# A graph network of three layers: twenty placed ranges per chunk instead of 22, and a second gather of 128 rows per four chunks

## The chip, the cores and the metric

The kernel runs on one core of one Trainium2 chip. The metric is the device time of one execution in microseconds; a smaller one is better. The engines are named as in the profile: PE (TensorE, matmuls, with PEld for its weight loads), DVE (VectorE), ACT (ScalarE), POOL (GpSimd, which issues the gathers here) and SP (SyncE, which issues the plain DMAs).

## The reference

6250 nodes with 64 features, 206250 edges sorted by their target node. Three layers of attention over the edges, a residual, and a final normalization:

```
for i in range(3):
    q, k, v = x @ Wq + bq, x @ Wk + bk, x @ Wv + bv
    e = edge_attr @ We
    alpha = sum(q[dst] * (k[src] + e)) / sqrt(64)
    p = exp(alpha - segment_max(alpha, dst)[dst])
    w = p / segment_sum(p, dst)[dst]
    x = relu(segment_sum((v[src] + e) * w, dst) + x @ Ws + bs)
    if i < 2: x = layer_norm(x)
out = layernorm(x_in + log_softmax(x))
```

The part that matters here is `x[src]`: for each edge, the row of 64 numbers of its source node.

## The kernel before

The edges are cut into 403 chunks of 512, a chunk into four tiles of 128 edges (`T = 4`), and four chunks make a batch (`LB = 4`), which is also the unit of work: 100 full batches and a rest. For each unit the program computes scores (`scores`, line 1641), exponentials (`exps`, ACT), transposes of the probabilities (`weights`, PE, then a copy to `probT`), and weighted sums (`sums`, line 1679).

The source rows of a chunk come in two ways. **By gather:** an indirect DMA on POOL fetches 128 rows of 64 numbers (`take`, line 592). **By matmul:** while the first layer runs, a sorter (`sorter`, `Move`) puts the edges of each chunk into a new order. The nodes are 49 blocks of 128. A chunk has a number of *ranges* (`WINDOWS`) of sixteen *places* (`SL`) each; range h holds only edges whose source lies in blocks 2h to 2h+3 (`BW = 4`). Edges that find no place in a range stand behind, in the order they had. With 22 ranges 352 places are filled so: tiles 0 and 1 wholly, and 96 rows (`PART`) of tile 2. In layers two and three the rows of placed edges are then selected by matmuls and not gathered:

- `Picker.aim` (line 1301): VectorE makes four one-hot tables `hot` from a key table (line 1313), for a pair of ranges and sixteen chunks (four batches, `TURN`).
- `Picker.bank` (line 1336): PE multiplies the node blocks `halves` with them, eight matmuls of 256 columns (line 1352); ACT casts the result into `kept` (line 1360). This is one *job*. `PAIRS` says how many pairs a layer has: 6 in the first layer, 11 in the others. Pair q is due with the batch k for which q % 4 == k % 4, so a batch has two or three jobs.
- `Picker.naturals` (line 1366): PE brings the selected rows into edge order, a matmul per tile and chunk with `kept` as weights (line 1387); DVE copies them to the batch's tile `feat`.

What is not placed is gathered (`rows_wanted`, line 575): per batch in layers two and three four gathers of tile 3, one per chunk, and one gather of 128 rows into `few` that serves the last 32 rows of tile 2 of all four chunks. `settle` (line 607) copies `few` into place on ACT, 32 rows per chunk. A gather's index is first copied to a small tile `gate` by ACT (`release`, line 631), which paces the gathers: those of batch u+2 are released at points inside unit u.

The order in each engine's queue is written by hand. A unit of layers two and three runs `scores` of the unit before, `naturals` of the next unit, one job, transposes of the rows (`turn`), the transposes of the probabilities, the remaining jobs, the sums, the settling copies.

The places come from `ranking` (line 892), four times, each for up to 112 chunks at once: one step per kind of source range, with four matmuls (line 927), an ACT copy with bias (931) and DVE operations. The first ranking must end before any chunk can be sorted. `REACH` bounds, per tile, the places that edges of this tile may take; the sorter's matmuls (lines 1063 and 1077) have this many columns. `Move.index` (line 1108) writes the node numbers of the edges to be gathered into `src_b`. A general computation (`general_path`) follows only if some chunk's edges don't fit the ranges or reaches.

Of the kernel before, what the change touches and what calls it, by code (L numbers as in the profile page):

```python
# [19 lines left out]
P = 128  # L20
# [16 lines left out]
WINDOWS = 22  # L37
# [14 lines left out]
REACH = (392, 416, 456, CH)  # L52
# [383 lines left out]
def main_path(  # L436
# [96 lines left out]
    assert 2 * (WINDOWS - 1) + BW < NB <= 2 * BINS and NT % TURN == 0 and U0 % TURN == 0 and REST * LB == P  # L533
# [22 lines left out]
    def fetch(layer, k):  # L556

        c0, m = batches[k]
        feat = feats.tile([P, LB * T * 2 * D], F32, name="feat")
        if placed(layer, k):  # L560
            nc.sync.dma_start(feat[:, LB * T * D :], eaP[k])
        if layer or placed(layer, k):
            feat = feat.rearrange("p (h c t d) -> p c t h d", h=2, c=LB, d=D)
        else:
            feat = feat.rearrange("p (c t h d) -> p c t h d", h=2, c=LB, d=D)
        if not placed(layer, k):
            nc.sync.dma_start(
                feat[:, :m, :, 1].rearrange("p c t d -> p (c t) d"),
                ea[c0 : c0 + m].rearrange("c (t p) d -> p (c t) d", p=P),
            )  # L570
        loaded[layer, k] = feat
        if layer and placed(layer, k):
            spares[layer, k] = later.tile([P, D], F32, name="few", bufs=FB + 1)

    def rows_wanted(layer, k):
# [6 lines left out]
        return [(None, 0)] + [(c, T - 1) for c in range(m)]  # L582

    def indices(layer, k, c, t):
# [3 lines left out]
        if c is None:  # L588
            return src_b, k * LB * T + (2 * LB - 1 if layer else LB + 1 + t // 2)
        return src_b, k * LB * T + t * LB + c  # L590

    def take(layer, k, c, t, index):

        nc.gpsimd.indirect_dma_start(  # L594
            out=loaded[layer, k][:, c, t, 0] if c is not None else spares[layer, k] if layer else loaded[0, k][:, t, 1, 0],
# [11 lines left out]
    def settle(layer, k):  # L607

        if layer and placed(layer, k):
            for c in range(LB):  # L610
                nc.scalar.copy(
                    loaded[layer, k][PART:, c, 2, 0], spares[layer, k][c * REST : (c + 1) * REST, :]
                )
# [396 lines left out]
    class Move:  # L1010
# [97 lines left out]
        def index(self):  # L1108
# [929 lines left out]
```

## Time and profile before

| what | us |
|---|---|
| median of 3 runs (4546.31 to 4551.62) | 4548.02 |
| the profiled execution, time | 4547.86 |
| the profiled execution, span from first to last instruction | 4546.1 |
| PE busy in the span (82%) | 3750.4 |
| DVE busy (68%) | 3110.5 |
| POOL busy (56%) | 2547.7 |
| ACT busy (54%) | 2434.5 |

The mean granted clock of TensorE is 0.895. A row of the groups view reads: source line, engine, operation, output<-inputs, shapes, count, then busy us and mean ns of one, then the idle time of the engine just before such instructions and what ended it. Matmuls overlap, so the busy time of a group divided by its count is less than the mean length of one. A row of the windows view gives, for one stretch, its length, the busy us of the five engine columns with the number of instructions, the granted clock, the share of the DMA engines' time and GB/s. In the timeline each row is a start, a duration, an engine and an operation.

### The profile page before, as it was taken

How to read it: one execution, taken by the hardware profiler on the slowest of the kernel's cores; microseconds unless marked ns; L12 is line 12 of the kernel's file. 1: busy time of each engine (PE TensorE's matmuls, PEld its weight loads, DVE VectorE, ACT ScalarE, POOL GpSimd, SP SyncE). 2: the span in 40 equal slices, each digit the busy share in tenths (PEclk: the TensorE clock that was granted, in tenths of full speed). 3: DMA queues.
4: the chain of work that ended last, by engine and by line, in shares of the span. 5: the costliest groups of instructions: out<-in, count | busy, mean ns of one | idle time of the engine just before them, and what ended most of it. 6: DMA issues, size and time to landing. Idle time of an engine off the chain costs nothing.

```text
span 4546.1 us, 106920 instructions
## 1 busy us (share of the span) xinstructions
PE 3750.4 (82%) x35698; PEld 2635.5 (58%) x35698; DVE 3110.5 (68%) x8905; ACT 2434.5 (54%) x6979; POOL 2547.7 (56%) x2094
## 2 busy tenths in 40 slices
PE   5778888888888888888789888888878888888885
PEld 2445555555555555555477666666747666666664
DVE  5566676776766766666477777777746777777784
ACT  2334544544545444544456666666645666666674
POOL 5545566666665665655265655565526655565653
PEclk9788998988989899998789999999878988899997
DMA  5446666667666677776467767777646776777774
GB/s 114 113 125 174 172 177 182 169 177 184 173 172 184 166 188 192 189 185 178 136 154 183 191 168 191 187 178 183 172 112 142 182 175 170 181 182 184 176 186 97
DMA packets 827547, 766.85 MB, mean 169 GB/s; under 512 B 395281, under 2 KB 624935, under 8 KB 826990
## 3 DMA queue, kind: packets, MB, share of 16 engines
q1 hardware_dynamic: 666370, 565.02, 49.8%
q0 software_dynamic: 66688, 68.42, 8.2%
q10 hardware_dynamic: 93932, 126.48, 7.9%
q8 instruction: 288, 4.72, 0.4%
q14 instruction: 269, 2.20, 0.2%
HBM read 599.30 MB, written 160.27 MB: 167 GB/s over the span
## 4 chain that ended last, share of the span: by engine, by line


## 5 line engine op out<-in xcount | busy, mean ns | idle before, releaser
L594 POOL DMA_INDIRECT feat<-in_x,gate x1044 | 1278.7, 1225 | 896.3 <-ACT gate L631 622.0
L1313 DVE TENSOR_SCALAR hot<-key,rank 128x512 fp32r<-128x512 f16 (+2 forms) x2832 | 1165.5, 474 | 144.4 <-DMA key<-keyS 34.6
L594 POOL DMA_INDIRECT feat<-x,gate x816 | 946.3, 1160 | 533.7 <-ACT gate L631 225.3
L1638 ACT COPY featT<-ps_a 64x512 f32<-64x512 f32 x1176 | 682.8, 581 | 86.3 <-remote 21.8
L1352 PE MATMUL ps_x<-hot,halves 128*128 128x256 f32 (+2 forms) x4368 | 684.1, 306 | 19.9 <-ACT kept L1360 9.0
L1352 PEld LDWEIGHTS ps_x<-hot,halves 128*128 128x128 f32 x4368 | 598.0, 202 | 31.8 <-ACT kept L1360 19.1
L1063 PE MATMUL ps_x<-hit,rest 128*64 128x512 bf16 (+3 forms) x3200 | 501.1, 391 | 11.0 <-issue 10.7
L1687 PE MATMUL ps_g<-feat,probT 128*32 128x128 f32 x9672 | 403.2, 295 | 117.7 <-issue 53.0
L594 POOL DMA_INDIRECT few<-x,gate x198 | 283.8, 1433 | 366.1 <-ACT gate L631 138.5
L1655 DVE TENSOR_REDUCE most<-ps_s 128x1 f32<-128x512 f32 x297 | 204.1, 687 | 391.3 <-PE ps_s L1648 156.6
L1052 DVE TENSOR_SCALAR hit<-ruler,pos 128x512 bf16<-128x512 f16 (+3 forms) x1600 | 421.6, 334 | 13.3 <-PE ps_m L1077 12.4
L1360 ACT CAST kept<-ps_x 128x512 fp32r<-128x512 f32 (+2 forms) x546 | 307.3, 582 | 218.1 <-PE ps_x L1352 137.0
L1648 PE MATMUL ps_s<-featT,q 128*32 128x512 f32 x2376 | 405.6, 640 | 11.2 <-issue 7.2
L1687 PEld LDWEIGHTS ps_g<-feat,probT 128*32 128x32 f32 x9672 | 287.1, 117 | 197.4 <-issue 104.5
L1635 PE MATMUL ps_a<-ident,feat 128*128 128x128 f32 x2348 | 353.1, 288 | 41.8 <-ACT gate L631 11.1
L1063 PE MATMUL ps_x<-hit,raw 128*64 128x512 bf16 (+3 forms) x1600 | 332.9, 404 | 8.0 <-issue 7.8
L631 ACT COPY gate<-src_b 128x1 int32<-128x1 int32 x1946 | 325.8, 191 | 20.7 <-ACT eN L1103 15.6
L1635 PEld LDWEIGHTS ps_a<-ident,feat 128*128 128x128 f32 x2348 | 288.6, 149 | 63.8 <-issue 23.2
L1387 PEld LDWEIGHTS ps_m<-twice,kept 128*128 128x128 f32 x1600 | 213.2, 206 | 186.9 <-issue 186.6
L1662 ACT ACTIVATE prob<-ps_s,part 128x512 f32<-128x512 f32 x297 | 204.3, 688 | 185.2 <-issue 33.2
L1063 PEld LDWEIGHTS <-rest 128*64 128x64 bf16 x3200 | 206.5, 123 | 162.3 <-issue 80.1
L1695 ACT COPY part<-ps_g 128x128 f32<-128x128 f32 (+1 forms) x309 | 82.6, 267 | 394.1 <-remote 124.9
(253 smaller groups left out, 5587.3 us busy)
## 6 DMA issues: line engine op xcount, KB each, us to landing
feat<-eaP SPq DMA_DIRECT2D x292, 512.0 KB
featT<-eaS SPq DMA_DIRECT2D x292, 512.0 KB
key<-keyS SPq DMA_DIRECT2D x668, 128.0 KB
raw<-in_ea SPq DMA_DIRECT2D x200, 256.0 KB
eaS<-eT ACTq DMA_DIRECT2D x200, 256.0 KB
eaP<-eN ACTq DMA_DIRECT2D x200, 256.0 KB
to<-toS SPq DMA_DIRECT2D x292, 128.0 KB
part<-part SPq DMA_DIRECT2D x600, 32.5 KB
```

The costliest lines, as they stand in the source:

```text
L594: nc.gpsimd.indirect_dma_start(out=loaded[layer, k][:, c, t, 0] if c is not None else spares[layer, k] if layer else loaded[0, k][:, t, 1, 0],
L631: copy(gate, index[:, i : i + 1])
L1052: nc.vector.tensor_scalar(hit, ruler[:, : REACH[t]], self.pos[:, at : at + 1], None, ALU.is_equal)
L1063: nc.tensor.matmul(self.px[i][j * D : (j + 1) * D, : REACH[t]], self.part(i, part)[:, (j * T + t) * D : (j * T + t + 1) * D], self.hits[t, ...
L1313: nc.vector.tensor_scalar(hot[:, a:b].rearrange("p k w e -> p (k w e)"), self.keys[job][:, a * 2 * SL : b * 2 * SL], rank[:, h : h + 1], None,
L1352: nc.tensor.matmul(px[:, w, a:b], halves[block >= EARLY][:, block - EARLY * (block >= EARLY)].rearrange("p h d -> p (h d)"), made[h][:, a: ...
L1360: nc.scalar.copy(kept[t][:, a:b, at : at + 2 * SL].rearrange("p k (w e) -> p w k e", w=2), px[:, :, a:b])
L1387: nc.tensor.matmul(pn[:, t - ts[0], c], kept[t][:, k % TURN * LB + c], twice, start=True, stop=True)
L1635: nc.tensor.transpose(pt[:, j - js[0], t // 2], rows[:, t * D : (t + 2) * D], ident)
L1638: nc.scalar.copy(featT[:, :, :, h, :], pt[h * D : (h + 1) * D])
L1648: nc.tensor.matmul(self.p_s[rows], self.q[:, j * STRIDE : j * STRIDE + W], self.featT[:, j, :], start=False, stop=True)
L1687: nc.tensor.matmul(p_g[rows, :].rearrange("n (h d) -> n h d", h=2), self.probT[:, t, rows], batch[:, c + j, t], start=(t == 0), stop=(t == ...
```

## The change

`WINDOWS` goes from 22 to 20, and what follows from it: 320 placed edges per chunk, 64 placed rows in tile 2 (`PART`), 64 rows to be gathered there (`REST`), ten pairs in layers two and three (`PAIRS`). `few` becomes two gathers' worth of rows, one gather of 128 rows for two chunks; the settling copies become two, each for two chunks; `index` writes one more column of node numbers per batch. The reaches are set anew.

```diff
-WINDOWS = 22
+WINDOWS = 20
...
-REACH = (392, 416, 456, CH)
+REACH = (376, 408, 464, CH)
...
-            spares[layer, k] = later.tile([P, D], F32, name="few", bufs=FB + 1)
+            spares[layer, k] = later.tile([P, LB // 2, D], F32, name="few", bufs=FB + 1)
...
-        return [(None, 0)] + [(c, T - 1) for c in range(m)]
+        return [(None, c) for c in range(0, m, 2)] + [(c, T - 1) for c in range(m)]
...
-            return src_b, k * LB * T + (2 * LB - 1 if layer else LB + 1 + t // 2)
+            return src_b, k * LB * T + LB + t // 2 + (LB // 2 if layer else 0)
...
-            out=loaded[layer, k][:, c, t, 0] if c is not None else spares[layer, k] if layer else loaded[0, k][:, t, 1, 0],
+            out=loaded[layer, k][:, c, t, 0] if c is not None else spares[layer, k][:, t // 2] if layer else loaded[0, k][:, t, 1, 0],
...
-            for c in range(LB):
-                nc.scalar.copy(
-                    loaded[layer, k][PART:, c, 2, 0], spares[layer, k][c * REST : (c + 1) * REST, :]
-                )
+            for i in range(2):
+                nc.scalar.copy(loaded[layer, k][PART:, i::2, 2, 0], spares[layer, k][i * REST : (i + 1) * REST])
...
-            pi = pa[:, : 3 + 2 * LB]
+            pi = pa[:, : 3 * LB]
...
-                at = 3 + (t - 2) * LB
+                at = (t - 1) * LB
...
+                rows = slice(c % 2 * REST, (c % 2 + 1) * REST)
+                at = (LB + c) // 2
                 nc.tensor.matmul(
-                    pi[c * REST : (c + 1) * REST, 2:3], self.to[:, SLOTS : 3 * P], pickc[:, c : c + 1], start=True, stop=True
+                    pi[rows, at : at + 1], self.to[:, SLOTS : 3 * P], pickc[:, c : c + 1], start=True, stop=True
                 )
             nc.vector.tensor_scalar(
-                src_b[:, k * LB * T + LB + 1 : (k + 1) * LB * T], pi, float(N - 1), None, ALU.min
+                src_b[:, k * LB * T + LB : (k + 1) * LB * T], pi, float(N - 1), None, ALU.min
             )
```

The rows below are the engines' programs in order, each with its line, operation, output<-inputs and output shape, repeated rows counted as x8. First PE in layer two, the last rows of a unit that prepares a batch with k % 4 == 2, before: two jobs (8 matmuls each, here over two halves of the node blocks) stand between the transposes of the probabilities (L1674) and the sums (L1687).

```order
L1648 MATMUL ps_s<-featT,q 32x512 x4
L1387 MATMUL ps_m<-twice,kept_254 128x64 x4
L1387 MATMUL ps_m<-twice,kept_32446 128x64 x4
L1387 MATMUL ps_g<-twice,kept_32447 96x64 x4
L1352 MATMUL ps_x<-hot,halves 128x256 x8
L1635 MATMUL ps_a<-ident,feat 128x128 x8
L1674 MATMUL ps_p<-ident,prob 128x128 x4
L1352 MATMUL ps_x<-hot,halves 128x256 x6
L1352 MATMUL ps_x<-hot,halves_32445 128x256 x10
L1687 MATMUL ps_g<-feat,probT 32x128 x16
```

The same place now:

```order
L1648 MATMUL ps_s<-featT,q 32x512 x4
L1387 MATMUL ps_m<-twice,kept_254 128x64 x4
L1387 MATMUL ps_m<-twice,kept_32350 128x64 x4
L1387 MATMUL ps_g<-twice,kept_32351 64x64 x4
L1352 MATMUL ps_x<-hot,halves 128x256 x8
L1635 MATMUL ps_a<-ident,feat 128x128 x8
L1674 MATMUL ps_p<-ident,prob 128x128 x4
L1352 MATMUL ps_x<-hot,halves 128x256 x6
L1352 MATMUL ps_x<-hot,halves_32349 128x256 x2
L1687 MATMUL ps_g<-feat,probT 32x128 x16
```

One job is left there, and the matmuls for tile 2 write 64 rows, not 96. In the other three of four units only the latter differs.

ACT in layer two, from the settling copies of one unit to those of the next, before (`gate` copies release gathers, `featT` are the copies behind `turn`):

```order
L611 COPY feat<-few 32x64 x4
L1662 ACTIVATE prob,part<-ps_s,part 128x512
L631 COPY gate<-src_b 128x1
L1360 CAST kept_254<-ps_x 128x2x16x16
L1638 COPY featT<-ps_a 64x4x128
L631 COPY gate<-src_b 128x1
L1638 COPY featT<-ps_a 64x4x128 x2
L631 COPY gate<-src_b 128x1
L1638 COPY featT<-ps_a 64x4x128
L1360 CAST kept_32446<-ps_x 128x2x16x16
```

The same stretch now:

```order
L611 COPY feat<-few 64x2x64 x2
L1662 ACTIVATE prob,part<-ps_s,part 128x512
L629 COPY gate<-src_b 128x1 x2
L1360 CAST kept_254<-ps_x 128x2x16x16
L1638 COPY featT<-ps_a 64x4x128 x2
L629 COPY gate<-src_b 128x1
L1638 COPY featT<-ps_a 64x4x128 x2
L629 COPY gate<-src_b 128x1
L1360 CAST kept_32350<-ps_x 128x2x16x16
```

Both gathers into `few` are now released at the unit's first point, and a gate copy more stands in the queue; POOL issues two gathers into `few` and four into `feat` per batch, where it issued one and four. The gathers of a layer's first batch have no gate and go one after the other: five before, six now.

More of the change, by code (lines that the diff above doesn't have):

```diff
@@ L532, in main_path @@
     U0 = LEAD
-    assert 2 * (WINDOWS - 1) + BW < NB <= 2 * BINS and NT % TURN == 0 and U0 % TURN == 0 and REST * LB == P
+    assert 2 * (WINDOWS - 1) + BW < NB <= 2 * BINS and NT % TURN == 0 and U0 % TURN == 0 and 2 * REST == P
     EARLY = -(-(2 * (2 * PAIRS[0] - 1) + BW) // GS) * GS
```

## The prediction

> **What bounds the kernel now.** I read the page's first part, then the busy times by stage, then the groups of TensorE, then single units of work.
>
> ```profile
> span 4546.1 us, 106920 instructions
> PE 3750.4 (82%) x35698; PEld 2635.5 (58%) x35698; DVE 3110.5 (68%) x8905; ACT 2434.5 (54%) x6979; POOL 2547.7 (56%) x2094
> ```
>
> The profiled execution took 4547.86 us, 1.8 us more than its span, and stands 0.16 us under the median of the runs shown; the sum below is made against 4547.9. PE leads with 82%, but the share is a mean over stages. The next view cuts the span at the layer boundaries; its columns are the stretch, its length, busy us of PE, PE's weight loads, DVE, ACT and POOL (instructions in brackets), granted clock, DMA share, GB/s.
>
> ```profile
> 300.00:2200.00 1900.00, 1583.07 (x15411) 976.14 (x15409) 1275.37 (x4052) 926.57 (x2662) 1142.03 (x922) 0.90 0.67 178
> 2200.00:2300.00 100.00, 77.56 (x534) 57.63 (x530) 51.86 (x172) 39.93 (x94) 15.50 (x9) 0.68 0.38 103
> 2300.00:3330.00 1030.00, 906.16 (x8937) 706.89 (x8937) 767.07 (x1914) 642.74 (x1877) 598.62 (x488) 0.93 0.73 180
> 3330.00:3440.00 110.00, 77.85 (x495) 59.68 (x493) 53.86 (x165) 40.34 (x113) 30.71 (x25) 0.64 0.39 95
> 3440.00:4440.00 1000.00, 851.97 (x8535) 677.35 (x8532) 743.40 (x1882) 647.03 (x1854) 576.21 (x473) 0.93 0.74 179
> ```
>
> In the first layer PE is busy 83% at clock 0.90. In the second and third (rows three and five, the stretches I call steady) it is busy 88% and 85% at 0.93, with DVE at 74%, ACT at 63%, POOL at 58%. The two changes of layer (rows two and four) run at 0.68 and 0.64: short, and chained. So PE is nearest to the end nearly everywhere, and an edit is worth mostly the PE work it removes, less what PE then waits longer. What PE does and waits for in the steady stretches:
>
> ```profile
> L1352 PE MATMUL ps_x<-hot,halves 128*128 128x256 f32 x4183 | 654.5, 305 | 19.9 <-ACT kept L1360 9.0 <-DVE hot L1313 7.3 <-issue 3.3
> L1687 PE MATMUL ps_g<-feat,probT 128*32 128x128 f32 x6200 | 248.2, 287 | 82.4 <-DVE probT L1677 47.3 <-issue 33.2 <-DVE hot L1313 0.8
> L1674 PE MATMUL ps_p<-ident,prob 128*128 128x128 f32 x780 | 128.3, 290 | 69.5 <-ACT prob L1662 64.4 <-issue 5.0
> ```
>
> The first row is the selection matmuls: 4183 took 654.5 us, so a job of eight takes 1.25 us, with hardly any waiting (19.9 us). The other two show where PE does wait: the transposes of the probabilities for ScalarE's exponentials (64.4 us), the sums for VectorE's copy of the transposed probabilities (47.3). A job stands just ahead of each; it is also cover for those waits, and that is what keeps its removal from paying in full.
>
> **Part 1: a selection job less per four batches.** Pairs of ranges per batch group fall from 11 to 10 in layers two and three. The pair removed belongs to every fourth group start, 26 times in a layer, 52 in all. Each takes with it eight matmuls (1.25 us of PE), four one-hot comparisons, a cast of the result and a key load. The kernel already holds the experiment: of four successive units three have three jobs and one has two, and afterwards it is two and two. I cut the steady stretches into units, at the first matmul of each unit's scores, and summed those with no node-finishing matmuls in them, the 30 two-job units first, the 85 three-job units second (first row, last row, sum):
>
> ```profile
> 2341.65:2349.69 8.04, 7.72 (x93) 5.93 (x85) 7.09 (x18) 6.11 (x20) 4.79 (x6) 1.00 0.89 226
> ...
> 4423.87:4432.47 8.60, 6.99 (x87) 5.92 (x89) 6.21 (x15) 5.76 (x19) 4.21 (x5) 1.00 0.71 181
> sum 287.45, PE 240.88 PEld 190.93 DVE 212.54 ACT 185.51 POOL 155.77; mean PE 8.03 PEld 6.36 DVE 7.08 ACT 6.18 POOL 5.19
> ```
>
> ```profile
> 2308.72:2320.28 11.56, 10.73 (x101) 8.65 (x92) 6.69 (x17) 6.49 (x20) 7.08 (x8) 0.85 0.63 154
> ...
> 4413.70:4423.87 10.17, 9.80 (x99) 6.94 (x91) 8.81 (x23) 6.54 (x21) 6.16 (x6) 1.00 0.74 173
> sum 894.08, PE 788.39 PEld 632.71 DVE 637.85 ACT 568.45 POOL 490.04; mean PE 9.28 PEld 7.44 DVE 7.50 ACT 6.69 POOL 5.77
> ```
>
> A unit takes 287.45/30 = 9.58 us with two jobs and 894.08/85 = 10.52 with three: 0.94 us for a job, of which PE's busy time (8.03 against 9.28) explains 1.25, so three quarters of the PE time removed comes back as time. With all 46 and 141 whole units, node-finishing ones too, the sums are:
>
> ```profile
> sum 446.32, PE 376.07 PEld 290.82 DVE 347.19 ACT 287.92 POOL 265.35; mean PE 8.18 PEld 6.32 DVE 7.55 ACT 6.26 POOL 5.77
> ```
>
> ```profile
> sum 1548.00, PE 1354.08 PEld 1071.78 DVE 1139.19 ACT 981.28 POOL 893.75; mean PE 9.60 PEld 7.60 DVE 8.08 ACT 6.96 POOL 6.34
> ```
>
> That is 9.70 and 10.98: 1.28 us a job. The three-job units hold more finishing steps (56 of 141 against 16 of 46), so I stay near the first: 1.0 us, **52 us** for 52 jobs, with ends 49 and 67. DVE's four comparisons, ACT's cast and the key load ran beside PE and are worth nothing more; they are inside the measured difference.
>
> **Part 2: narrower natural-order matmuls.** The third tile's placed part shrinks from 96 to 64 columns of weights, for 800 matmuls in layers two and three. The first layer does the same operation with 64 already:
>
> ```profile
> L1387 PE MATMUL ps_g<-twice,kept 128*96 128x64 f32 x800 | 108.8, 262 | 13.1 <-ACT part L1695 8.4 <-issue 4.4 <-DVE sk L1432 0.2
> L1376 PE MATMUL ps_p<-twice,kept 128*64 128x64 f32 x368 | 36.9, 223 | 1.6 <-issue 1.6
> ```
>
> 108.8/800 = 0.136 us against 36.9/368 = 0.100: 0.036 x 800 = 29 us of PE. At three quarters, as in part 1, **22 us** (ends 0, if all of it turns into waiting for the exponentials behind it, and 29). The copy to SBUF that follows keeps its length per partition, so it costs the same.
>
> **Part 3: fewer ranking steps.** Each of four rankings counts 21 kinds, not 23. The first ranking stands ahead of all sorting; five steps of it in this stretch (PE of that line alone):
>
> ```profile
> 86.60:97.20 10.60, 6.51 (x20) 3.20 (x20) 1.00 0.31 70
> ```
>
> 20 matmuls in 10.60 us: a step takes 2.1 us there and 1.30 us of PE. In the first ranking the steps form a chain over PE, ACT and DVE, so two fewer give 4.2 us whole. The six others lie beside other work: 6 x 1.30 x 0.75 = 6. Together **10 us** (4 to 12).
>
> **Part 4: the reaches of the products.** The widths per tile go from 392, 416, 456, 512 to 376, 408, 464, 512: 16 columns fewer in 1776.
>
> ```profile
> L1063 PE MATMUL ps_x<-hit,rest 128*64 128x392 bf16 x800 | 105.3, 339 | 1.5 <-issue 1.3
> L1063 PE MATMUL ps_x<-hit,rest 128*64 128x456 bf16 x800 | 121.1, 375 | 5.6 <-issue 5.4
> ```
>
> 15.8 us for 64 columns over 800 matmuls; the undivided words add half as many matmuls. 15.8 x 1.5 x 16/64 = 6 us of PE, at three quarters **4 us** (0, and 10 if time is proportional to the width).
>
> **Part 5: the sorter a move earlier.** With four fewer steps in the first ranking, moves begin earlier: in the program order two moves are left after the first layer's loop, not three counted from its last unit's scores. The tail runs with idle PE:
>
> ```profile
> 2190.00:2220.00 30.00, 21.32 (x199) 11.06 (x198) 9.75 (x37) 9.54 (x20) 5.29 (x5) 0.75 0.33 109
> 2260.00:2290.00 30.00, 24.89 (x101) 21.73 (x102) 21.01 (x67) 8.57 (x19) 7.25 (x5) 0.50 0.34 83
> ```
>
> In the first row PE idles 8.7 us of 30. I take **3 us** (0 to 8.7).
>
> **Part 6: a sixth gather per batch, and its gate and settling copies.** 200 more gathers of 128 rows on POOL.
>
> ```profile
> L594 POOL DMA_INDIRECT feat<-x,gate x816 | 946.3, 1160 | 533.7 <-ACT gate L631 225.3 <-issue 149.3 <-ACT feat L611 134.9
> L594 POOL DMA_INDIRECT few<-x,gate x198 | 283.8, 1433 | 366.1 <-ACT gate L631 138.5 <-DVE feat L1394 72.3 <-PE ps_x L1352 44.3
> ```
>
> A unit's POOL time goes from 4 x 1.16 + 1.43 = 6.1 us to 7.5, in units of 9.6 to 11. The gathers released in a unit feed the unit after the next, so 1.4 us later is hidden by a whole unit; I cost them at nothing there. If that cover were gone, PE would wait for rows. At the two changes of layer there is no such lead: the six gathers of the first batch go one after the other, and the last ones end PE's wait:
>
> ```profile
> 2287.08 6.41 DVE L1313 TENSOR_SCALAR hot<-key,rank 128x512 fp32r<-128x512 f16 x16
> 2286.80 6.82 POOL L594 DMA_INDIRECT feat<-x,src_b  x1 [0.30 <-issue]
> 2295.96 0.33 PE L1635 MATMUL ps_a<-ident,feat 128*128 128x128 f32 x1 [1.55 <-DMA feat<-x,src_b]
> ```
>
> The fifth gather here took 6.82 us, beside sixteen one-hot comparisons that VectorE ran without a break from 2287.08 for 6.41 us; TensorE then waited 1.55 us for its rows. A sixth adds one gather length, 1.16 to 1.43 us, at each change of layer: **-2.5 us** (0, since the last job before it is gone as well, to -8 if two are caught by the comparisons). The Trainium skill's "SBUF — State Buffer", section "Who interferes with whom", says that a VectorE operation in a two-port mode locks GpSimd out of a shared port for its whole length, and that software descriptors wait for it; the row of 6.82 us agrees. Nothing of the sum hangs on it.
>
> ScalarE: four settling copies become two of twice the length.
>
> ```profile
> L611 ACT COPY feat<-few 32x64 f32<-32x64 f32 x800 | 193.2, 241 | 18.9
> L631 ACT COPY gate<-src_b 128x1 int32<-128x1 int32 x1946 | 325.8, 191 | 20.7 <-ACT eN L1103 15.6 <-issue 4.1 <-ACT eT L1091 0.9
> L1695 ACT COPY part<-ps_g 128x128 f32<-128x128 f32 x300 | 80.4, 268 | 384.3 <-remote 124.9 <-PE ps_s L1648 66.2 <-PE ps_g L1687 54.2
> ```
>
> Two copies of 128 elements at about 0.268 (the nearest row of that length) replace four of 0.241: 0.43 us less; one gate copy more: 0.19. The copies stand ahead of the exponentials, which PE waits for in some units, so I take **2 us** (0 to 5). DMA carries 128 rows of 256 bytes more per unit and a quarter of a key load less (the row below: 128 KB each); at a share of 0.73 I cost it at nothing, with the prefetch of later units as cover.
>
> ```profile
> key<-keyS SPq DMA_DIRECT2D x668, 128.0 KB
> ```
>
> **The sum.** 52 + 22 + 10 + 4 + 3 + 2 - 2.5 = 90.5 us: 4547.9 - 90.5 = 4457. All upper ends: 67 + 29 + 12 + 10 + 9 + 5 = 132, 4416. All lower ends: 49 + 4 - 8 = 45, 4503.
>
> **Where the clock could take it back.** Granted clock follows PE's busyness: of the two rows of part 5 the one that is 71% busy ran at 0.75, the other, between layers, at 0.50. So lighter units could fall to the slow clock more often. The unit rows bear on it: the mean of the clock column is 0.92 over the 30 two-job units and 0.93 over the 85 three-job ones, so a job less does not lower it, and the sum goes by that. The Trainium skill ("TensorE: Matmul & The Clock Gate", section "What's actually happening") states a gate that halves the clock after an idle window of about 3.4 us and has only two states. By that rule a lighter unit could be slower; it is the first rival.
>
> **The rivals.** (a) The clock drops: the steady stretches hold 906.16 + 851.97 = 1758 us of PE work at 0.93. At 0.884 this would grow by 91 us and cancel the gain; that is where it decides. At 0.86 it grows by 143 and the kernel ends at 4600, slower than before. Against it: the two means above. (b) Gathers come late: if the 1.55 us wait of the layer change struck in 59 of the 200 units it would cancel the gain; in all of them it costs 310 us, 4767. For it: POOL would be busy 7.5 of some 10 us, and comparisons stretch single gathers. Against it: the lead of a unit, and a third fewer comparisons in one unit of four. (c) The freed PE time becomes waiting: the 64.4 and 47.3 us waits grow, a job is worth 0.63 us (half), the narrower weights nothing: 33 + 10 = 43 us less, 4505. For it: those waits stand behind what is removed. Against it: the two-job units pay 0.94. (d) The change does not do what it says: if an edge found no place, the general computation would run after this one, an estimate of another 4500 us or more. Working the ranking out on the reference's edges with 20 ranges, every chunk fills its ranges (smallest slack 0, as with 22) and the reaches leave 13 places or more, so this is all but excluded.
>
> **How the numbers follow.** Runs agree to about 0.1%, so 0.2% (9 us) is about what can be told from no change. The forecast with its ends (4416 to 4490): 0.74. (c), up to 4539: 0.15. (a) 0.03, (b) 0.03, (d) 0.01; something between, within 0.2%: 0.04. Faster: 0.74 + 0.15 = 0.89; slower 0.07. The range reaches from all upper ends, 4415, past (c) to 4525.
>
> **What would show it.** Right: selection matmuls 416 fewer at 0.156 us each; natural matmuls near 0.10 us; units of the steady stretches shorter by about 0.4 us in the mean; clock 0.92 or more there; a first ranking shorter by some 4 us; POOL nearer to 70%. Wrong: a clock under 0.9 in the steady stretches (a); PE waiting for gathered rows in most units (b); the waits on exponentials and transposed probabilities doubled (c).

## The result, and the profile after

The changed kernel takes 4849.55 us (median of 4 runs, 4838.94 to 4854.48) against 4547.17 for the kernel before on the same chip: 1.0682 times as long, interval [1.0642, 1.0721]. The prediction was 4457. The profiled execution took 4849.07 us. Two lines of its page:

```profile
span 4847.3 us, 105185 instructions
PE 3814.4 (79%) x35250; PEld 2631.6 (54%) x35250; DVE 3028.8 (62%) x8663; ACT 2351.3 (49%) x6715; POOL 2601.6 (54%) x2294
```

There are 448 matmuls fewer, as planned (416 selections and 32 of the rankings), and PE is nevertheless busy 64 us longer. The windows of the changed kernel, one row for each layer without its ends (the last two are the steady stretches):

```profile
300.00:2300.00 2000.00, 1600.93 (x15356) 972.70 (x15357) 1271.97 (x4034) 921.37 (x2643) 1026.03 (x915) 0.88 0.64 168
...
2410.00:3540.00 1130.00, 918.75 (x8714) 710.76 (x8717) 725.53 (x1795) 602.76 (x1752) 687.44 (x584) 0.86 0.66 163
...
3660.00:4740.00 1080.00, 887.71 (x8321) 677.61 (x8320) 708.94 (x1783) 610.82 (x1732) 644.66 (x567) 0.87 0.68 165
```

In layers two and three PE is busy 81 and 82%, not 88 and 85, at clock 0.86 and 0.87, not 0.93. DVE, ACT and the DMA engines are all less busy as well, and POOL is at 61 and 60%: none of these has become a new bound, they wait. The time from the first to the last exponentials of a layer was 2125.9, 1083.3 and 1072.8 us before and is 2234.3, 1191.7 and 1159.0 now: about 100 us in each layer, also in the first, whose gathers the change doesn't touch. The changes of layer did not grow.

Who waits is seen in the groups view over layers two and three: first two groups of the kernel before (2300 to 4440 us), then the changed one (2410 to 4740 us).

```profile
L1655 DVE TENSOR_REDUCE most<-ps_s 128x1 f32<-128x512 f32 x193 | 132.5, 687 | 148.0 <-PE ps_s L1648 95.7 <-PE ps_m L1387 17.6 <-PE ps_x L1352 12.2
L1695 ACT COPY part<-ps_g 128x128 f32<-128x128 f32 (+1 forms) x196 | 52.7, 269 | 252.1 <-remote 102.6 <-PE ps_s L1648 61.5 <-PE ps_s L1646 43.1
```

```profile
L1352 PE MATMUL ps_x<-hot,halves 128*128 128x256 f32 (+1 forms) x3844 | 631.0, 315 | 26.0 <-ACT kept L1360 18.7 <-issue 7.1
L1687 PE MATMUL ps_g<-feat,probT 128*32 128x128 f32 x6200 | 275.4, 304 | 147.9 <-DVE probT L1677 102.4 <-issue 43.3 <-DVE hot L1313 0.7
L1674 PE MATMUL ps_p<-ident,prob 128*128 128x128 f32 x784 | 135.9, 301 | 72.9 <-ACT prob L1662 63.0 <-issue 9.7
L1655 DVE TENSOR_REDUCE most<-ps_s 128x1 f32<-128x512 f32 x193 | 132.9, 689 | 305.7 <-PE ps_s L1648 163.9 <-PE ps_m L1387 51.3 <-PE ps_a L1635 45.3
L1387 PE MATMUL ps_g<-twice,kept 128*64 128x64 f32 x776 | 85.3, 237 | 29.0 <-ACT part L1695 25.7 <-issue 3.2
L1695 ACT COPY part<-ps_g 128x128 f32<-128x128 f32 (+1 forms) x196 | 52.5, 268 | 384.0 <-remote 120.9 <-PE ps_s L1648 93.7 <-PE ps_m L1387 92.7
```

VectorE's wait for the scores (L1655) doubled, from 148 to 306 us, and PE's wait for the copy `probT` (L1687) grew to 102.4. The row to dwell on is the last. ScalarE's copy `part` has only to wait for the sums of its own unit, `ps_g` L1687. Yet what released it were `ps_s` L1648 and `ps_m` L1387, matmuls that PE runs *after* those sums, or "remote", something that the profile doesn't show. PE's own record says that the sums were done; ScalarE heard of it later. It waited 252 us so before, and 384 now. (The trace models the ends of matmuls, so what follows rests on delays much longer than one matmul. Two engines agree through a semaphore: the first increments it when an instruction is done, the second waits for the value. I call the increment a mark, and a late one the lag.) The timeline shows one such stall, in a unit with two jobs:

```profile
3478.57 1.03 POOL L594 DMA_INDIRECT feat<-x,gate  x1 [0.30 <-ACT prob L1662]
...
3479.63 0.60 PE L1674 MATMUL ps_p<-ident,prob 128*128 128x128 f32 x4
3479.90 0.99 POOL L594 DMA_INDIRECT feat<-x,gate  x1 [0.30 <-DMA featT<-eaS]
...
3479.98 1.21 PE L1352 MATMUL ps_x<-hot,halves 128*128 128x256 f32 x8
...
3481.20 0.94 POOL L594 DMA_INDIRECT feat<-x,gate  x1 [0.30 <-issue]
...
3482.45 0.94 POOL L594 DMA_INDIRECT few<-x,gate  x1 [0.30 <-issue]
...
3483.69 0.94 POOL L594 DMA_INDIRECT few<-x,gate  x1 [0.30 <-issue]
...
3484.94 0.94 POOL L594 DMA_INDIRECT feat<-x,gate  x1 [0.30 <-issue]
...
3486.19 0.94 POOL L594 DMA_INDIRECT feat<-x,gate  x1 [0.30 <-issue]
3488.13 0.69 DVE L1677 COPY probT<-ps_p 128x512 f32<-128x512 f32 x1 [7.36 <-remote]
...
3488.87 1.51 PE L1687 MATMUL ps_g<-feat,probT 128*32 128x128 f32 x24 [7.68 <-DVE probT L1677]
```

PE's transposes L1674 end at 3480.23 by their records. VectorE, idle, starts the copy that waits for them only at 3488.13, 7.9 us later. In between POOL runs gathers without a pause, about 0.94 us each and 0.30 apart; the last one ends at 3487.13, and the mark arrives about 1 us later. The semaphore's events in the trace say the same: PE's marks in this stall came at 3480.26, 3481.71, 3481.74, 3483.15, 3484.55 and 3488.11, no more than one or two in a gather and none in the last two, and then four at 3488.83, .87, .90 and .93, 0.03 to 0.04 apart, for matmuls that were 0.12 apart and recorded as done by 3481.19.

This holds for the whole trace. In layer two of the kernel before (2420 to 3300 us) PE's marks come at 0.35 to 1.3 per us in the first 1.4 us after a gather's start, while it runs and just behind, and at 2.7 to 4.0 per us in the 1.2 us after that, as long as no other gather has begun. The trace keeps 6473 marks of 7933 instructions that make one, so the rates are a little low; but it is not only that marks are missing: the matmuls that make them end evenly, at 2.1 per us within gathers and in those 1.2 us, so marks that are short in the first are made good in the second. The other direction shows no such delay: where PE stood waiting in layers two and three, it started 0.05 us after the end of the copy `probT` and 0.14 after that of the exponentials (medians), in gathers as outside.

### The profile page after: what moved, and what is told of

Read it like the earlier page. It is cut to its first block, busy times and chain, and to the rows that moved or that the text cites. A ratio compares the mean times of both kernels' runs of the same rounds, so it can differ in the third digit from the quotient of the medians.

```text
span 4847.3 us, 105185 instructions
## 1 busy us (share of the span) xinstructions
PE 3814.4 (79%) x35250; PEld 2631.6 (54%) x35250; DVE 3028.8 (62%) x8663; ACT 2351.3 (49%) x6715; POOL 2601.6 (54%) x2294
## 4 chain that ended last, share of the span: by engine, by line
## 5 line engine op out<-in xcount | busy, mean ns | idle before, releaser
L594 POOL DMA_INDIRECT feat<-in_x,gate x1044 | 1168.0, 1119 | 1127.0 <-ACT gate L629 785.2
L1313 DVE TENSOR_SCALAR hot<-key,rank 128x512 fp32r<-128x512 f16 (+2 forms) x2624 | 1090.7, 477 | 188.8 <-remote 58.9
L594 POOL DMA_INDIRECT feat<-x,gate x816 | 851.9, 1044 | 512.6 <-ACT gate L629 315.1
L594 POOL DMA_INDIRECT few<-x,gate x396 | 542.1, 1369 | 415.7 <-ACT gate L629 329.2
L1352 PE MATMUL ps_x<-hot,halves 128*128 128x256 f32 (+1 forms) x3952 | 648.5, 316 | 26.0 <-ACT kept L1360 18.7
L1687 PE MATMUL ps_g<-feat,probT 128*32 128x128 f32 x9672 | 441.1, 314 | 215.7 <-DVE probT L1677 112.2
L1655 DVE TENSOR_REDUCE most<-ps_s 128x1 f32<-128x512 f32 x297 | 204.8, 689 | 648.2 <-PE ps_s L1648 304.3
L1352 PEld LDWEIGHTS ps_x<-hot,halves 128*128 128x128 f32 x3952 | 568.0, 212 | 29.9 <-ACT kept L1360 20.4
L1687 PEld LDWEIGHTS ps_g<-feat,probT 128*32 128x32 f32 x9672 | 310.4, 124 | 305.0 <-DVE probT L1677 122.3
L1648 PE MATMUL ps_s<-featT,q 128*32 128x512 f32 x2376 | 428.9, 664 | 17.2 <-issue 13.6
L1360 ACT CAST kept<-ps_x 128x512 fp32r<-128x512 f32 (+1 forms) x494 | 281.5, 581 | 253.4 <-remote 133.5
L629 ACT COPY gate<-src_b 128x1 int32<-128x1 int32 x2144 | 349.7, 190 | 93.8 <-ACT eT L1089 41.9
L1360 ACT CAST kept<-ps_g 128x512 fp32r<-128x512 f32 (+2 forms) x142 | 81.6, 574 | 542.0 <-remote 149.4
L1387 PEld LDWEIGHTS ps_m<-twice,kept 128*128 128x128 f32 x1600 | 220.4, 211 | 206.4 <-issue 204.5
```

The source lines that it names most:

```text
L594: nc.gpsimd.indirect_dma_start(out=loaded[layer, k][:, c, t, 0] if c is not None else spares[layer, k][:, t // 2] if layer else loaded[0, ...
L629: copy(gate, index[:, i : i + 1])
L1313: nc.vector.tensor_scalar(hot[:, a:b].rearrange("p k w e -> p (k w e)"), self.keys[job][:, a * 2 * SL : b * 2 * SL], rank[:, h : h + 1], None,
L1352: nc.tensor.matmul(px[:, w, a:b], halves[block >= EARLY][:, block - EARLY * (block >= EARLY)].rearrange("p h d -> p (h d)"), made[h][:, a: ...
L1360: nc.scalar.copy(kept[t][:, a:b, at : at + 2 * SL].rearrange("p k (w e) -> p w k e", w=2), px[:, :, a:b])
L1387: nc.tensor.matmul(pn[:, t - ts[0], c], kept[t][:, k % TURN * LB + c], twice, start=True, stop=True)
```

## The experiments

These runs fell on five chips, with the kernel before beside them: in the order of this text it took 4560, 4500, 3841, 3843 and 4551 us there. The chips differ, so ratios are compared, each to the kernel before on its own chip; lengths of layers are of one profiled execution each.

**The four suspects one by one** (kernel before 4560 us). First a sixth gather added to the kernel before:

```diff
...
-        return [(None, 0)] + [(c, T - 1) for c in range(m)]
+        return [(None, c) for c in range(0, m, 2)] + [(c, T - 1) for c in range(m)]
...
```

> The kernel before with 22 ranges, plus a second gather of 128 rows per batch in layers two and three, into the second half of a wider `few` tile. It fetches the same rows again, so nothing else changes: same jobs, same widths, same sorter. Units of the kernel before take 20.75, 10.61 and 10.70 us in the three layers, those of the changed kernel 21.84, 11.71 and 11.51. Theory G (the sixth gather makes the units of layers two and three wait for landings): layer one stays at 20.75, layers two and three grow by 0.8 to 1.1 us a unit, the whole to 4700-4770 us. Theory C (fewer matmuls let the clock fall, the gather is harmless): within 20 us of 4547, clock as before, 0.895. Theory R (reaches or the order of the sorter): likewise within 20 us.

4858.3 us, ratio 1.0614 [1.054, 1.0688]. Layers 2163.3, 1227.3 and 1200.7 us, against the trace of before on its chip: the first, which the edit doesn't touch, 37 longer, the others 144 and 128. ScalarE's wait for the sums is that of the changed kernel:

```profile
L1695 ACT COPY part<-ps_g 128x128 f32<-128x128 f32 (+1 forms) x196 | 52.4, 268 | 383.8 <-remote 164.0 <-PE ps_s L1648 76.6 <-PE ps_m L1387 76.5
```

The sixth gather alone makes layers two and three slow. Next it is taken out of the changed kernel, so that chunks three and four get the rows of the first two and theirs are left out:

```diff
-        return [(None, c) for c in range(0, m, 2)] + [(c, T - 1) for c in range(m)]
+        return [(None, 0)] + [(c, T - 1) for c in range(m)]
...
```

> The changed kernel without its second gather into `few`: chunks three and four of a batch get the rows of the first two for the 64 last places of tile 2, so their rows there are left out; five gathers per batch as before the change, all else as in the changed kernel. Theory G: layers two and three fall to 10.2-10.5 us a unit, layer one stays at 21.84, the whole at 4580-4640. Theory C: layers two and three stay at 11.5-11.7, the whole at 4820-4850. If the slow part of layer one has the same root, it stays in all cases here, since layer one's gathers are untouched.

4629.2 us, 1.0121 [1.0058, 1.0184]; layers 2263.9, 1084.1, 1044.2. Layers two and three are back, layer one isn't. Two edits aim at it:

```diff
-REACH = (376, 408, 464, CH)
+REACH = (392, 416, 456, CH)
```

> The changed kernel with the reaches of before (392, 416, 456, 512): only the widths of the sorter's products, codes and comparisons differ. Theory R1 (the new widths cost something in layer one, for instance by where a 464-wide matmul ends): layer one back from 21.84 to 20.8 us a unit, the whole near 4740. The others: within 10 us of 4850.

4896.6 us, 1.0695 [1.0621, 1.0769], layer one 2258.7: the widths are not it. And, at the end of `ranking`, four turns in which the sorter does nothing:

```diff
+        for _ in range(4):
+            yield
         left = sorts.tile([P, CH], FP16, name="order", bufs=1)[:n]
```

> The changed kernel with four empty turns at the end of each ranking, so that the sorter starts its moves at the same unit as before the change (45 index steps at unit 45, not 46); the work is that of the changed kernel. Theory R2 (the sorter one move ahead puts its pieces at worse places of layer one): layer one back to 20.8 us a unit, the whole near 4740, layers two and three unchanged at 11.7 and 11.5. The others: within 10 us of 4850.

4760.7 us, 1.0417 [1.0355, 1.0479]; layers 2125.3, 1212.1, 1169.5. Layer one is whole again. So the loss has two parts: the sixth gather, and the sorter one move early. In layer one the wait that grew and went back is that of ScalarE's copy of a job's result; the rows are before (300 to 2200 us), changed (300 to 2300), and with the four turns (300 to 2200):

```profile
L1360 ACT CAST kept<-ps_g 128x512 fp32r<-128x512 f32 (+2 forms) x136 | 79.0, 581 | 228.4 <-PE ps_m L1101 64.2 <-remote 63.8 <-PE ps_a L1124 35.0
```
```profile
L1360 ACT CAST kept<-ps_g 128x512 fp32r<-128x512 f32 (+1 forms) x137 | 79.6, 581 | 528.1 <-remote 144.5 <-PE ps_m L1075 132.9 <-PE ps_a L1099 111.8
```
```profile
L1362 ACT CAST kept<-ps_g 128x512 fp32r<-128x512 f32 (+2 forms) x136 | 78.9, 580 | 243.1 <-remote 96.4 <-PE ps_m L1101 50.9 <-PE ps_a L1126 41.8
```

**What of a gather costs?** (kernel before 4500 us.) First, in `take`, behind the last gather of a batch, the same gather again into a tile that nothing reads; second, in its place, two index ramps on POOL; third, the changed kernel with four turns and an earlier release (the line below stands in two places), and fourth the kernel before with that release:

```diff
+        if layer and placed(layer, k) and c == LB - 1:
+            scrap = later.tile([P, D], F32, name="scrap", bufs=FB + 1)
+            nc.gpsimd.indirect_dma_start(out=scrap, ...)
```
```diff
...
+            for _ in range(2):
+                scrap = later.tile([P, CH], FP16, name="scrap", bufs=2)
+                nc.gpsimd.iota(scrap, pattern=[[1, CH]], ...)
```
```diff
-            lead = 2 * LB if not layer else min(2 * LB, LB + u)
+            lead = 2 * LB if not layer else min(2 * LB + 2, LB + u)
```

> The kernel before (22 ranges), with the fourth gather of tile 3 of each batch in layers two and three issued a second time, with the same indices, into a scrap tile that nothing reads. No copy into a gate and no settling is added, and nothing waits for its rows. The version whose sixth gather was read took 4858 us. Theory L (the sixth gather is a matter of rows that come too late for those who need them, the scrap ones only push the others): 4600-4700, less than with the gather early in the batch. Theory D (every gather costs the other engines time while its descriptors are made or its rows move, whoever reads them): 4820-4870. If what costs is the gate copy or the settling on ScalarE: 4550-4570.

> The kernel before, with two index ramps of 128x512 on POOL (0.55 us each in the profile) behind the last gather of each batch in layers two and three, written to a tile that nothing reads: POOL is as long busy as with a sixth gather, but no descriptor is made and no row moves. Theory P (POOL's time or its use of SBUF is what costs): near 4850. Theory D (descriptors and transfers): within 20 us of 4550. Theory L: 4600-4850, as the gathers behind are later by as much.

> The changed kernel with four empty turns per ranking (4760.7 us measured) and, in layers two and three, every gather released two chunks, half a unit, earlier. Theory L: the units of layers two and three fall from 11.96 and 11.62 to 10.2-10.6 us, the whole to 4480-4560. Theories P and D: they stay above 11.4, the whole at 4720-4770.

> The kernel before with the gathers of layers two and three released half a unit earlier. Theory L: if five gathers already cost something by being late, faster than 4550 by up to 60 us; else the same. Theories P and D: within 20 us of 4550.

The gather that nothing reads: 4694.6 us, 1.0412 [1.0303, 1.0521]. The ramps: 4477.4, 0.9992 [0.9951, 1.0033]. The earlier release: 4698.7, 1.0446 [1.0357, 1.0535], where without it the same kernel stood at 1.0417 on the other chip. The kernel before with it: 0.9989 [0.9953, 1.0025]. The POOL rows of the first two:

```profile
L602 POOL DMA_INDIRECT scrap<-x,gate x198 | 206.1, 1041 | 60.6 <-issue 59.1 <-DVE hot L1321 0.6 <-PE ps_a L1643 0.3
```
```profile
L603 POOL IOTA scrap<- 128x512 f16 x400 | 251.1, 658 | 1.7
```

The ramps hold POOL for 251 us and cost nothing; the gathers hold it for 206 and cost 185 us (0.0412 x 4500), though nobody waits for their rows. By itself that cost lies between the theories: L had 50 to 150 us, D 270 to 320. The other two decide: a later POOL queue costs nothing, earlier gathers gain nothing, and both speak against L and P. The gate and the settling can make up no more than the step from 4.1 to 6.1%, which also lies between two chips. The bulk is something that a gather does to others.

It does not show in every wait, though. The next rows are ScalarE's copies in layers two and three on this chip, first with the ramps (2310 to 4390 us), then with the scrap gather (2320 to 4620):

```profile
L1364 ACT CAST kept<-ps_x 128x512 fp32r<-128x512 f32 (+1 forms) x530 | 298.5, 582 | 136.6 <-PE ps_x L1356 95.0 <-remote 23.1 <-PE ps_a L1639 7.9
L1699 ACT COPY part<-ps_g 128x128 f32<-128x128 f32 (+1 forms) x197 | 52.5, 267 | 285.4 <-remote 92.6 <-PE ps_s L1650 80.9 <-PE ps_s L1652 73.5
```
```profile
L1368 ACT CAST kept<-ps_x 128x512 fp32r<-128x512 f32 (+1 forms) x530 | 298.3, 582 | 313.8 <-PE ps_x L1360 180.6 <-remote 81.6 <-PE ps_p L1682 26.7
L1703 ACT COPY part<-ps_g 128x128 f32<-128x128 f32 (+1 forms) x197 | 52.6, 267 | 226.9 <-remote 78.8 <-PE ps_s L1656 57.2 <-PE ps_s L1654 40.1
```

The wait for the sums is shorter in the slower run, and in the kernel before with the earlier release it is 87.6 us (2310 to 4470 us) at an unchanged time. So this wait is a sign of late marks and not a measure of what they cost. What grew with the scrap gather is ScalarE's wait for the jobs (`kept`), PE's wait for `probT` (26.8 to 89.0 us), and the time at half clock: 587 us against 273, from the first exponentials of layer two to the last of layer three.

**Rows, traffic, and the rest of the change** (kernel before 3841 us). A scrap gather of 16 rows (`index[: P // 8]`); a plain DMA of 128 rows in its place (`nc.sync.dma_start(scrap, xts[layer][:P, :])`); the changed kernel with five gathers and four turns; the changed kernel with eight turns.

> The kernel before with a sixth gather that nothing reads, as in the run where it cost 4.1%, but of 16 rows, not 128. Theory D1 (it costs by the instruction, or by POOL's work of making descriptors as long as its length stays): if POOL's gather still takes some 1 us, +3 to +4%; if it takes an eighth, under +1%. Theory D2 (it costs by the rows moved): an eighth of 4.1%, so within 1% of before, whatever POOL's length.

> The kernel before with a plain DMA of 128 rows of 256 bytes per batch in layers two and three, issued by SP into the scrap tile: the traffic of a sixth gather without descriptors made on POOL. Theory D2 (the traffic): +3 to +4%. Theory D1 (making descriptors on POOL): within 0.5% of before.

> The changed kernel with five gathers per batch (chunks three and four of a batch get the rows of the first two for the last 64 places of tile 2, so their rows there are left out) and the sorter at its old place by four empty turns: everything of the change but its sixth gather and the shift of the sorter. If the terms of the prediction other than parts 5 and 6 hold (52 + 22 + 6 + 4 + 2 us), it stands 1.9% under before. From the two single removals (4629 and 4761 against 4850) it should stand 4540, 0.4% under before. So: 0.2 to 0.6% under if those two are all, 1.5 to 2% if the prediction's terms are whole.

> The changed kernel with eight empty turns per ranking: the sorter two moves later than in the changed kernel, one later than before the change. If the phase of the sorter against the jobs (period of two or four units) makes layer one slow, it may go either way here: near 22 us a unit if odd shifts are slow, near 20.7 if only the changed kernel's phase is. If it is a matter of being early, 20.7 or less. The whole: 4850 or 4750.

Ratios: 1.0096 [1.0066, 1.0125], 1.0033 [1.0014, 1.0052], 0.9849 [0.9815, 0.9884], 1.005 [1.003, 1.0071]. These can't be set beside the earlier ones: this chip runs the kernel before 700 us faster. So the changed kernel itself ran next, to be compared on another chip, with the two scrap kernels again and, last, a pause on POOL (a ramp of 128x256) behind every gather of the kernel before.

> The changed kernel itself, beside the kernel before on this call's chip. Theory H (TensorE's marks to other engines are held back while POOL makes descriptors, on some chips only): on a chip where the kernel before takes about 4550 us, 6 to 7% slower, and the marks lag in its trace; on one where it takes about 3850 us, within 1% of before and no lag. Theory D without H (a gather costs some 1.4 us by itself): 5 to 7% slower on any chip.

> The kernel before with a sixth gather of 16 rows that nothing reads. Its POOL time was 1.22 us, as long as one of 128 rows, and it cost 1.0% on the chip of 3841 us. On a slower chip: theory H, +3 to +4.5%, as 128 rows cost there; theory of rows (each row's descriptors or transfer): +0.3 to +1%. On a chip of about 3850 us: +1% again.

> The kernel before with the plain DMA of 128 rows per batch issued by SP; +0.33% on the chip of 3841 us. Theory H: the same 0 to 0.5% on a slower chip. If traffic is what costs there: +3 to +4%.

> The kernel before with a pause on POOL behind every gather of layers two and three, an index ramp of 128x256 (about 0.35 us), so that gathers never follow each other at 0.3 us. Theory H: if held marks drain in the pauses, faster than before by 0.5 to 3% on a slower chip; if they wait for the end of all queued gathers whatever the pauses, the same. On a chip without the lag: 0 to 1% slower.

Kernel before 3843 us. The changed kernel: 3903.0, 1.0149 [1.011, 1.0189], where within 1% was expected. 16 rows: 1.008 [1.0058, 1.0102]; plain DMA: 1.0024 [0.9999, 1.005], not run on a chip with the lag. The pauses: 1.0391 [1.0353, 1.0429], where 0 to 1% was expected; the ramps hold POOL for 469 us, and PE waits 37.1 us for gathered rows in layers two and three, against 3.9 with the plain DMA. Whether pauses help where marks are late was not seen. The windows of the changed kernel here (one row a layer), and the wait for the sums over 1990 to 3780 us:

```profile
300.00:1880.00 1580.00, 1401.78 (x15111) 887.14 (x15106) 1235.87 (x3957) 895.73 (x2620) 1045.66 (x902) 0.94 0.80 210
1990.00:2830.00 840.00, 744.95 (x8345) 604.25 (x8344) 682.11 (x1711) 566.02 (x1665) 651.24 (x553) 0.96 0.85 210
2970.00:3780.00 810.00, 710.52 (x8095) 581.77 (x8087) 677.26 (x1735) 582.29 (x1676) 633.43 (x544) 0.96 0.87 213
```
```profile
L1695 ACT COPY part<-ps_g 128x128 f32<-128x128 f32 (+1 forms) x193 | 51.9, 269 | 32.1 <-PE ps_g L1687 28.9 <-PE ps_s L1646 0.5
```

The same program: 32.1 us of waiting, not 384.0, and released by its own sums, L1687. PE's marks come at 2.1 to 2.4 per us while a gather runs (2420 to 3300 us), no slower than outside. There is no lag on this chip, and the sixth gather and the shift together cost 3.0% on the two chips without it (1.0149 against 0.9849), not the 8.3% of the two removals above (1.0682 less 1.0121, and 1.0682 less 1.0417).

**Is it the gathers that make the lag?** (kernel before 4551 us.) In layers two and three every gather becomes a plain DMA from SP of the first 128 rows of x, so that the rows wanted are left out; layer one keeps its own. Beside it the 16 rows once more.

```diff
+        if layer and placed(layer, k):
+            nc.sync.dma_start(
+                loaded[layer, k][:, c, t, 0] if c is not None else spares[layer, k], xts[layer][:P, :]
+            )
+            return
```

> The kernel before, with each of the five gathers per batch of layers two and three replaced by a plain DMA of 128 rows issued by SP (always the first 128 rows of x, so the gathered rows are left out); same jobs, same bytes, but POOL makes no descriptors there. Layer one keeps its gathers. Theory H on a chip of about 4550 us: the copies of the sums start within 0.1 us of TensorE's end in layers two and three, their units fall from 10.6 to about 9 us, the whole by 300 to 340 us (6.5 to 7.5%), layer one stays at 20.7. On a chip of about 3850 us: units from 9.1-9.2 to 8.5-9, 1 to 4% faster. If the slower chips are slow for another reason (transfers, the clock): units stay above 10 us, under 3% faster.

> The kernel before with a sixth gather of 16 rows that nothing reads. On a chip of about 4550 us: +3 to +4.5% if the lag goes by the instruction's time on POOL, +0.3 to +1% if by its rows. On a chip of about 3850 us: +0.8 to +1% for the third time.

16 rows: 4752.9 us, 1.042 [1.0321, 1.052], as much as 128 rows cost on the chip of 4500. With plain DMAs: 4455.8, 0.978 [0.9709, 0.9851]. ScalarE's wait for the sums in that run, first in layer one (300 to 2200 us, gathers), then in layers two and three (2350 to 4400, none), and the POOL row of the other:

```profile
L1700 ACT COPY part<-ps_g 128x128 f32<-128x128 f32 x91 | 24.2, 266 | 121.8 <-PE ps_m L1082 36.2 <-PE ps_g L1692 35.7 <-remote 27.2
```
```profile
L1700 ACT COPY part<-ps_g 128x128 f32<-128x128 f32 (+1 forms) x199 | 53.6, 269 | 39.5 <-PE ps_g L1692 26.8 <-remote 7.9
```
```profile
L602 POOL DMA_INDIRECT scrap<-x,gate x198 | 198.7, 1003 | 62.6 <-issue 62.0 <-DVE hot L1321 0.6
```

In one execution the lag is there in layer one, with its gathers, and gone in the other two: 39.5 us for 199 copies, against 252.1 for 196. PE's marks in layer one come at 0.83 per us in the first us of a gather and at 3.42 from 1.4 to 2.6 us after its start; in layer two, without gathers, at 2.14 throughout. So the gathers make the lag. A gather of 16 rows is as long on POOL as one of 128 and costs as much, so the cost goes by the instruction, not by its rows or their traffic. But theory H's size was wrong: it expected 6.5 to 7.5%, and got 2.2, which lies where the expectation put a chip that is slow for another reason. So it is not shown that the lag makes up the 700 us between the chips, nor how much of a gather's price goes through it. Slower transfers are not the other reason: packets of 4 KB on the busiest DMA queue took 159 ns (median) in the changed kernel on both kinds of chip. Layers two and three took 1026.1 and 1005.6 us, not the 930 and 897 of the kernel with one plain DMA more, on a chip without the lag (`scrap_sp2`). A part of that is a new wait, of a kind that the kernel before doesn't have here:

```profile
L1653 PE MATMUL ps_s<-featT,q 128*32 128x512 f32 x1568 | 215.4, 620 | 124.0 <-DMA featT<-eaS 104.9 <-ACT feat L616 10.0 <-ACT gate L636 4.6
```

The scores wait 104.9 us for the transposed edge features, which SP issues as it does the five new DMAs of each batch; that these hold them up is likely and not shown. The rest, about 100 us, is about what a slower clock adds to PE's work: for the same matmuls it is busy 1784 us here and 1683 in `scrap_sp2`, from the first exponentials of layer two to the last of layer three, and at half clock for 403 us, not 188. What slows the clock there with the lag gone stays open.

## Why the prediction was wrong, point by point

- **Part 6, the gathers in steady units: the step that failed.** It asked only when rows are needed ("hidden by a whole unit") and costed 200 gathers at nothing. The rows were indeed not late: releasing them half a unit earlier bought nothing. But on this chip TensorE's marks come late while POOL works on a gather. Taking the sixth gather out of the changed kernel gave 5.6% of the kernel before (1.0682 to 1.0121, 255 us), adding it to the kernel before cost 6.1% (1.0614, 280 us of 4560), some 1.3 to 1.4 us for each of 200. That the gather costs this is shown; that the late marks carry the whole of it is not. A sign stood in the trace of before: 252 us of waiting in one ScalarE copy, released by matmuls that come later in PE's program. I had read PE's waits and not those of the engines that wait for PE.
- **Part 6, the changes of layer.** Costed at -2.5 us. From the last exponentials of a layer to the first of the next it took 57.2 and 59.3 us before, 55.9 and 56.6 after: a small gain.
- **Part 5, the sorter.** Forecast as a gain of 3 us at the end of layer one. The changed kernel's units of that layer are 1.07 us longer in the mean (2125.9 and 2234.3 us in 101 steps); four empty turns took 109 us of it back (2234.3 to 2125.3). I had looked at the tail, where two moves less remain, and not at the 90 units in which the moves now meet other work. That it is the shift is shown; why one move earlier is bad and one later isn't (1757.1 us with eight turns, 1760.6 with four, against 1808.3 without any, all on chips without the lag) is not. The wait of the copies `kept` for their jobs is longer by it with the lag and without: on the chips without, 220.2 us against 145.5 with eight turns.
- **Parts 1 and 2, jobs and narrower matmuls.** Their counts came as forecast: L1352 has 403 fewer in the window (4247 before). Their durations didn't quite: at the lower clock a matmul of L1352 takes 631.0/3844 = 0.164 us, not 0.156, so the group lost 33 us of PE time and not 63, and L1387 takes 85.3/776 = 0.110 us, not 0.100. Their worth was mis-sized. On the chip without the lag the change less its two losses is 1.51% faster, 58 us of 3841, where parts 1 to 4 and ScalarE's 2 us made 86 without the first ranking's 4; on a chip with the lag layers two and three of the version with one `few` gather are 28 us shorter than before (2128.3 against 2156.1, one execution each, on two chips), of 74. Why a job less is worth so little there is not shown; that it gives more waiting for marks is a guess. The three quarters were taken from the two-job units, in which all else was as before.
- **Part 3.** The first ranking took 63.9 us, from the first to the last of its matmuls, and 66.4 before: 2.5 us, not 4.2.
- **Part 4.** The old reaches give the same ratio (1.0695 against 1.0682): below what can be told.
- **The range.** The lower ends of the terms add up to 4503, and the prediction ends its forecast at 4490 without a reason; 4849.55 is far outside both.
- **The rivals.** (a), the clock, came as described, 0.86 and 0.87 in the steady stretches, and is a large part of the loss there: from the first exponentials of layer two to the last of layer three TensorE had half its clock for 707 us of 2407, against 399 of 2216 before. But where it can be followed it came behind a wait: in the stall shown above PE stood still from 3481.2, and the clock was 1.00 until 3484 and 0.50 from there. The prediction's paragraph on the clock also misread its two rows: the one at clock 0.50 had the busier PE, 24.89 of 30 us or 83%, against 71% at 0.75, so they don't show that the clock follows the busy share. (b) came nearest in size (4767) by luck, with the wrong mechanism: earlier rows gained nothing. (c) was half right: the wait for `probT` grew from 47.3 to 102.4 us, that for the exponentials did not (64.4 and 63.0). That late marks could stand behind (a) and (c) was in none of them.

## What to carry to other kernels

Look not only at what an engine waits for but at who waits for it: if a copy is released by matmuls that come after its producer, or by "remote", the signal was late, and the list of PE's own waits will not show it. But don't take the length of such a wait for its price; take the time of a run that leaves the cause out. Before adding a gather on POOL that nobody has to wait for, try one that nothing reads: here a sixth one per unit outweighed all that the change saved, and 16 rows cost as much as 128. And a schedule written by hand has a phase: an edit that shortens a side task by two steps may move it against the main loop for a whole layer, so the count of side steps is changed together with the loop or padded back.

## What the runs showed of the hardware that was not expected

- While POOL works on a gather, TensorE's marks reach other engines late, on some chips: 0.35 to 1.3 per us against 2.7 to 4.0 just after. A ramp on POOL does not do it: during the ramps marks came at 3.0 per us (2420 to 3300 us), as behind a gather. The engines' own operations go on: VectorE starts 1.7 to 1.9 per us during a gather and 2.0 to 2.1 later, and PE's matmuls start at 9 to 10 per us. The Trainium skill ("SBUF — State Buffer", section "Who interferes with whom") says that PE and ACT never wait on anyone; on SBUF ports that may stand, but these traces show engines that hear from PE late while GpSimd works on a gather (7.9 us in the stall above). Whether the mark alone is held or PE's last step too, the trace can't tell.
- Chips differ: the same kernel took 4500 to 4560 us on those with the lag and 3841 to 3843 on those without, and the same change 1.068 and 1.015 times as long. A ratio from one chip is not a property of the kernel.
- A gather of 16 rows holds POOL as long as one of 128, 1.00 us against 1.04 in the two runs with the lag.
